# A four-layer graph kernel on one core: rounds per block in the dilation, batch 0's attention beside its preparation, and the order of high and low halves in layer 1

## The chip, the cores and the metric

The kernel runs on one core of a Trainium2 chip. A core has TensorE (PE, matrix products into PSUM), VectorE (DVE), ScalarE (ACT), GpSimd (POOL) and SyncE (SP, which here only issues DMAs). The metric is device time of one execution in microseconds (us); the number that counts is the median of several runs.

## What is computed

Input: features x of 16 batches, 1024 nodes, 128 columns; symmetric 0/1 adjacencies of 16 x 1024 x 1024 with a full diagonal and about 6% ones; a node mask of ones. Each of four layers is a residual and a layer norm, `x = layernorm(x + layer(x, adj))`. The three that matter here:

Layer 0, a gated attention. The score is symmetric, so one product with a fixed matrix gives it.

```python
h = x @ W_w.T + W_b
e = einsum('bjl,bkl->bjk', h @ A, h);  e = e + swapaxes(e, 1, 2)
att = softmax(where(adj > 0, e, -9e15), axis=1) * adj
h_prime = relu(einsum('bij,bjk->bik', att, h))
coeff = sigmoid(concatenate([x, h_prime], -1) @ gate_w.T + gate_b)
return coeff * x + (1 - coeff) * h_prime
```

Layer 1 first thins the adjacency ("dilation"), row after row, each row seeing what earlier rows removed:

```python
def step(carry, n):
    row = carry[n]; num = row.sum()
    sf = where(num > 10, (num + 1) // 2, 1)
    rm = row & (cumsum(row) % sf == 0) & (num > 1)
    carry = carry.at[n].set(row & ~rm)
    carry = carry.at[:, n].set(carry[:, n] & ~rm)
```

and then applies three graph convolutions `out = (adj_d @ x / deg) @ Wr + x @ Wx + b`, each normalized by rows and over the batch. Layers 2 and 3 (a second gated attention and a graph convolution) are not touched by the change.

## The kernel before, in words

**One program, static order.** Everything is unrolled Python that issues instructions to five engines through a tile framework. The framework sets the waits, and it also places the instructions of an engine: the order in the program acts as a priority, and the trace shows instructions of a later stream ahead of those of an earlier one where their inputs are ready. Streams of work are Python generators. `take_turns` (L811) steps several of them alternately; `in_rounds` (L815) steps each one when it is due, and a value that it yields is the number of rounds that it then pauses.

**Layer 0.** `before(s, b)` (L923) prepares a batch: it loads the features xn (L926) and, in eight steps `it`, a block of 128 adjacency rows each (L931), converts it to fp8 on ScalarE (L932, the tile named carry), and checks that the adjacency is symmetric and binary on VectorE (L937, and L945 on PE's transposes, L944). Beside this, at `it == 2` it turns xn into xT (PE L759, ScalarE L951); at `it == 4` it makes G, the scores' right-hand side (PE L766, ScalarE L955, with M0, a product of raw weights made at L894 to L909), and the gate's first half (L775, L777, L780, L958); at `it == 5` it makes hn (PE L963, VectorE L964). `attention(s, b)` (L968) takes eight column blocks: mask (ScalarE L981), score product (PE, called at L982, recorded at L724), masked minimum (VectorE L984), exponential (ScalarE L986), scaling by the sum (L988, L990), and one block later the product with the weights (PE L974). `after(s, b)` (L999) gates and normalizes, and stores. Batch 0's preparation has a call of `in_rounds` of its own (L1024); then batch b's attention runs with batch b+1's preparation and batch b-1's `after` (L1025 to L1032). The raw weights lie in a pool that is opened and closed (L894) on the same side of SBUF on which the work pool is opened next (L910). The PSUM pool ps_h (L892) has two buffers, shared by the weights' products, the transposes and all products of the preparation.

**The dilation.** The 1024 rows are cut into eight blocks k of 128, the 16 batches into two groups g of eight: 16 steps in the order k0g0, k0g1, k1g0 and so on. Within a block the rows depend on each other, so `fixed_point` (L1080) solves for the counts by iteration. One evaluation (L1090) is: thr (L1092), mid = (sk == thr), over 128 x 1024 elements (L1097), eight column sums on PE (pd, L1100), and the new counts ti (L1104); for the last two blocks also even (L1095) and eight more sums (L1102). EVALS, 6 for all blocks, is the number of evaluations. Afterwards VectorE compares the last two iterates (L1107, tile bad) and writes negc, posc and wid, the last at L1130. `removal` (L1133) then applies one batch's block: ranks by products with a step matrix (PE L1144, L1142), two ScalarE passes (L1145), keep (VectorE L1148, L1149), and the mirror of the new rows into the columns (PE L1152 to L1156, ScalarE L1157). `prepare` (L1048) makes sk for the same group's next block. `take_turns` runs the fixed point of step i beside the eight removals of step i-1 and the `prepare` of step i+1 (L1190 to L1193). The first fixed point runs beside the last batch's `after` (L1174).

**The flag.** At the end bad and other conditions are reduced to one number; if it is not zero, a second, general kernel runs (L1842).

**Layer 1.** PE multiplies fp32 features in two passes: `split` (L1268) makes hi, a rounded copy (ScalarE L1272), and lo, the rest (VectorE L1273); lo has a single buffer. `widened` (L1286) makes eight pieces of the adjacency, alternately by ScalarE (L1295) and VectorE (L1293). `adjacency_product` (L1298) has two halves h of 512 columns; for each of a half's four pieces it issues two products with hi, then two with lo (L1306). It is called once in `first` (L1415) for each batch, and once in `keep` (L1482) for each batch in the first two convolutions: 48 times.

Of the kernel before, what the change touches and what calls it, by code (L numbers as in the profile page):

```python
# [17 lines left out]
OP = mybir.AluOpType  # L18
# [6 lines left out]
BIG = 2.0 ** 53  # L25
LN_EPS = 1e-5
BN_EPS = 1e-5
EVALS = 6
GB = 8
QB = 4  # L30

# [608 lines left out]
def fast_kernel(ctx: ExitStack, tc: tile.TileContext, t: dict, out: bass.AP, flag: bass.AP):  # L640

    nc = tc.nc
    B, N, D = t["x"].shape
    NT = N // P
# [42 lines left out]
    def nat(ap):  # L687
        return ap.rearrange("(t p) d -> p t d", p=P)
# [12 lines left out]
    def matrix(pool, src, name, bufs=1):  # L701
        v = pool.tile([P, P], F32, name=name, bufs=bufs)
        nc.sync.dma_start(v, src)
        return v

    def transposed(pool, psum, src, name, tag="tr"):
        v = pool.tile([P, P], F32, name=name)
        p = psum.tile([P, P], F32, name="wtr", tag=tag)
        nc.tensor.transpose(p, src, identf)
        nc.vector.tensor_copy(v, p)  # L710
        return v
# [16 lines left out]
    def tiles3(ap):  # L728
        return ap.rearrange("p (t d) -> p t d", d=P)
# [85 lines left out]
    def in_rounds(streams):  # L815

        due, r = [0] * len(streams), 0
        while any(streams):
            for i, s in enumerate(streams):
                if s is not None and due[i] <= r:  # L820
                    pause = next(s, 0)
                    if pause == 0:
                        streams[i] = None
                    else:
                        due[i] = r + (pause or 1)
            r += 1
# [64 lines left out]
    ps_a = ending.enter_context(tc.tile_pool(name="l0_pa", bufs=1, space=PSUM, reuse_waits="tile"))  # L891
    ps_h = ending.enter_context(tc.tile_pool(name="l0_ph", bufs=2, space=PSUM, reuse_waits="tile"))  # L892

    with tc.tile_pool(name="l0_raw", bufs=1) as raw:  # L894
        W0 = matrix(raw, t["L0_gnn_W_w"], "l0W")
        W0T = transposed(wts, ps_h, W0, "l0WT", "h")
        As0 = symmetric(raw, ps_h, matrix(raw, t["L0_gnn_A"], "l0A"), "l0As", "h")
        AW = raw.tile([P, P], F32, name="l0AW")
        p = ps_h.tile([P, P], F32, name="wtr", tag="h")
        nc.tensor.matmul(p, As0, W0, start=True, stop=True)  # L900
        nc.vector.tensor_copy(AW, p)
        M0 = wts.tile([P, P], F32, name="l0M")
        p = ps_h.tile([P, P], F32, name="wtr", tag="h")
        nc.tensor.matmul(p, W0, AW, start=True, stop=True)
        nc.vector.tensor_copy(M0, p)
        nu = wts.tile([P, 1], F32, name="l0nu")
        p = ps_h.tile([P, 1], F32, name="wtr", tag="h")
        nc.tensor.matmul(p, AW, column(raw, t["L0_gnn_W_b"], "l0b"), start=True, stop=True)
        nc.vector.tensor_scalar(nu, p, -1.0, None, op0=OP.mult)  # L909
# [6 lines left out]
        nc.sync.dma_start(gw[:, :, 0], t["L0_gnn_gate_w"].rearrange("o (h d) -> d (o h)", d=P))  # L916
    gb = row_bcast(wts, t["L0_gnn_gate_b"], 1, "l0gb")
    gbh = wts.tile([P, 1], F32, name="l0gbh")
    nc.vector.tensor_scalar(gbh, gb, 0.5, None, op0=OP.mult)
    nbig = wts.tile([P, 1], F32, name="l0nbig")  # L920
    nc.vector.memset(nbig, BIG)

    def before(s, b):  # L923

        s.xn = work.tile([P, NT, P], F32, name="xn", bufs=3)
        nc.sync.dma_start(s.xn, nat(t["x"][b]))  # L926
        yield 1
        for it in range(NT):
            c = b * NT + it
            an = early.tile([P, N], F32, name="an", bufs=3)  # L930
            nc.sync.dma_start(an, t["adj"][b][it * P:(it + 1) * P, :])  # L931
            nc.scalar.activation(Y[b][:, it, :], an, AF.Copy, accum_out=deg[:, c:c + 1], saturate=False)  # L932

            chk = early.tile([P, N], FP8, name="chk")
            done = (it + 1) * P
            if done < N:
                nc.vector.scalar_tensor_tensor(chk[:, done:], an[:, done:], 0.0, an[:, done:], op0=OP.is_gt,  # L937
                                               op1=OP.not_equal, accum_out=other[:, b, it:it + 1], saturate=False)
            for h in range(it // 4 + 1):
                js = range(4 * h, min(4 * h + 4, it + 1))  # L940
                k = slice(js[0] * P, (js[-1] + 1) * P)
                pt = ps_h.tile([P, 512], F32, name="pt", tag="h")
                for i, jt in enumerate(js):
                    nc.tensor.matmul(pt[:, i * P:(i + 1) * P], Y[b][:, jt, it * P:done], identb, start=True, stop=True)  # L944
                nc.vector.scalar_tensor_tensor(chk[:, k], pt[:, :k.stop - k.start], 0.0, an[:, k], op0=OP.is_gt,  # L945
                                               op1=OP.not_equal, accum_out=other[:, b, 7 + it + 4 * h:8 + it + 4 * h],
                                               saturate=False)
            if it == 2:
                s.xT = work.tile([P, N], F32, name="xT", bufs=2)
                for p, c, _ in turned(ps_h, s.xn):  # L950
                    nc.scalar.copy(s.xT[:, c], p)  # L951
            elif it == 4:
                s.G = work.tile([P, N], F32, name="G", bufs=2)
                for p, c in products(ps_h, (M0, s.xT)):
                    nc.scalar.activation(s.G[:, c], p, AF.Identity, scale=-1.0, bias=nu)  # L955
                pz = gates(ps_h, early.tile([P, N], FP8, name="chk").bitcast(F32), (gw[:, 0, :], s.xT))
                s.gx = small.tile([P, NT], F32, name="gx")
                nc.vector.tensor_copy(s.gx.rearrange("p (q t) -> p q t", t=2), pz[:, :, :, 0])  # L958
            elif it == 5:
                s.hn = work.tile([P, N], F32, name="hn")  # L960
                for p, c, blocks in halves(ps_h):
                    for i, k in enumerate(blocks):
                        nc.tensor.matmul(p[:, i * P:(i + 1) * P], s.xT[:, k * P:(k + 1) * P], W0T, start=True, stop=True)  # L963
                    nc.vector.tensor_add(tiles3(s.hn[:, c]), tiles3(p), b0[:, None, :].to_broadcast([P, 4, P]))  # L964
            yield 2
        nc.gpsimd.dma_start(adj8_d[b], Y[b].bitcast(F32))
# [54 lines left out]
        yield  # L1021

    state = [Batch() for _ in range(B)]
    in_rounds([before(state[0], 0)])  # L1024
    for b in range(B):  # L1025
        streams = []
        if b < B - 1:
            streams.append(before(state[b + 1], b + 1))
        streams.append(attention(state[b], b))
        if b:  # L1030
            streams.append(after(state[b - 1], b - 1))
        in_rounds(streams)  # L1032
    scores.close()

    with ExitStack() as ph:
# [44 lines left out]
        def fixed_point(st, k, g):  # L1080
# [6 lines left out]
            nc.vector.tensor_scalar(v1m, l1, 0.5, -0.5, op0=OP.mult, op1=OP.add)  # L1087
            ti = tiny.tile([P, GB], I32, name="ti")
            nc.vector.tensor_copy(ti, v1m)
            for e in range(EVALS):  # L1090
                thr = tiny.tile([P, GB], I32, name="thr")
                nc.vector.tensor_scalar(thr, ti, 1, None, op0=OP.bitwise_or)  # L1092
                if st.with_last:
                    even = tiny.tile([P, GB], BF16, name="even")
                    nc.vector.tensor_tensor(even, thr, ti, op=OP.is_equal)  # L1095
                mid = sb.tile([P, GB, P], FP8, name="mid")
                nc.vector.tensor_tensor(mid, st.sk, per_member(thr), op=OP.is_equal, saturate=False)  # L1097
                pd = ps_d.tile([P, GB], F32, name="pd")
                for i in range(GB):
                    nc.tensor.matmul(pd[:, i:i + 1], mid[:, i, :], onec, start=True, stop=not st.with_last)  # L1100
                    if st.with_last:
                        nc.tensor.matmul(pd[:, i:i + 1], st.last[:, i, :], even[:, i:i + 1], start=False, stop=True)  # L1102
                tn = tiny.tile([P, GB], I32, name="ti")
                nc.vector.tensor_tensor(tn, pd, v1m, op=OP.add)  # L1104
                prev, ti = ti, tn
                yield
# [151 lines left out]
    with ExitStack() as ph:  # L1258
# [39 lines left out]
        def adjacency_product(pieces, parts):  # L1298

            for h in range(H2):  # L1300
                acc = ps_a.tile([P, 512], F32, name="acc")
                for i in range(NT // 2):
                    for p, part in enumerate(parts):
                        for j in range(2):
                            jt = 2 * i + j
                            nc.tensor.matmul(acc, part[:, jt, :], pieces[h * NT // 2 + i][:, j, :],  # L1306
                                             start=(jt == 0 and p == 0), stop=(jt == NT - 1 and p == 1))
                yield acc, slice(h * 512, (h + 1) * 512)

        def home(b):  # L1310
# [178 lines left out]
        before = None  # L1489
# [5 lines left out]
        for l in range(3):  # L1495
# [42 lines left out]
            before = step  # L1538
# [7 lines left out]
    with ExitStack() as ph:  # L1546
# [7 lines left out]
        W2T, b2, As2, gw, gb, nbig, blcol, Wl = l2.W2T, l2.b2, l2.As2, l2.gw, l2.gb, l2.nbig, l2.blcol, l2.Wl  # L1554
# [247 lines left out]
        state = l2.state  # L1802
# [63 lines left out]
```

## Time and profile before

| | |
|---|---|
| median of 3 runs | 2735.02 us (2731.83 to 2736.03) |
| the profiled execution's own time | 2734.11 us |
| its span, first to last instruction | 2732.4 us |
| mean granted TensorE clock | 0.976 |
| busy: PE, PEld, DVE, ACT, POOL | 93%, 62%, 77%, 72%, 12% |
| layer 0 | 0 to about 649 us |
| dilation (first to last L1097, then the last removals) | 649.9 to about 1022 us |
| layer 1 | to about 1680 us |
| layers 2 and 3 | to the end |

How to read it: the profile shows one execution. "PE" is TensorE's products, "PEld" its loads of weights, which overlap them. A group line names the source line, the engine, the operation, output and inputs; behind the bar stand busy time, mean duration, idle time of that engine just before such instructions, and what ended it. A line of a stretch gives, after its ends and length, the busy us of PE, PEld, DVE, ACT and POOL, the granted clock, the DMA share and GB/s. A line of the timeline gives start, duration, engine, source line, operation, output and inputs, count, and in brackets the idle time before it and who ended it.

### The profile page before, as it was taken

How to read it: one execution, taken by the hardware profiler on the slowest of the kernel's cores; microseconds unless marked ns; L12 is line 12 of the kernel's file. 1: busy time of each engine (PE TensorE's matmuls, PEld its weight loads, DVE VectorE, ACT ScalarE, POOL GpSimd, SP SyncE). 2: the span in 40 equal slices, each digit the busy share in tenths (PEclk: the TensorE clock that was granted, in tenths of full speed). 3: DMA queues.
4: the chain of work that ended last, by engine and by line, in shares of the span. 5: the costliest groups of instructions: out<-in, count | busy, mean ns of one | idle time of the engine just before them, and what ended most of it. 6: DMA issues, size and time to landing. Idle time of an engine off the chain costs nothing.

```text
span 2732.4 us, 41821 instructions
## 1 busy us (share of the span) xinstructions
PE 2552.2 (93%) x15048; PEld 1688.8 (62%) x15048; DVE 2108.6 (77%) x5650; ACT 1977.0 (72%) x3188; POOL 317.1 (12%) x287
## 2 busy tenths in 40 slices
PE   7999999994899888998999998999999999999986
PEld 3444444442666657887778887456666666666655
DVE  5887778875999986776678877577787787787785
ACT  6888889873888786666655543777777777777773
POOL 0000000003000001121112123001010010001001
PEclk9999999996999999999999999999999999999998
DMA  5455445430000042233356655101222211111100
GB/s 189 162 169 171 165 167 177 157 114 23 2 2 2 2 183 96 94 108 124 132 203 224 254 205 211 39 24 62 70 77 73 90 62 62 62 62 62 46 24 25
DMA packets 120810, 285.38 MB, mean 104 GB/s; under 512 B 12305, under 2 KB 65425, under 8 KB 113425
## 3 DMA queue, kind: packets, MB, share of 16 engines
q1 hardware_dynamic: 101280, 203.33, 22.4%
q0 software_dynamic: 19312, 79.28, 7.5%
q8 instruction: 121, 1.98, 0.3%
q14 instruction: 97, 0.79, 0.1%
HBM read 202.72 MB, written 79.82 MB: 103 GB/s over the span
## 4 chain that ended last, share of the span: by engine, by line
PE 62%; DVE 16%; issue 9%; POOL 5%; ACT 4%; DMA 3%; SPq 0%; POOLq 0%; ACTq 0%; DVEq 0%
PE acc L974 8%; PE ph L1618 8%; PE pmm L724 8%; PE acc L1678 7%; PE ph L766 6%; PE acc L1306 5%; PE ph L759 4%; PE pmm L1690 3%; POOL rn L745 2%; PE ph L1605 2%; PE ph L1432 2%; DVE mid L1097 2%; POOL ln_rstd L745 1%; PE s L1144 1%; DVE keep L1148 1%
## 5 line engine op out<-in xcount | busy, mean ns | idle before, releaser
L745 POOL TENSOR_TENSOR ln_rstd<-ln_rstd,mhalf 128x8 f32<-128x8 f32 (+1 forms) x68 | 108.3, 1592 | 1347.6 <-DVE ln_rstd L742 879.7
L974 PE MATMUL acc<-em,hs 128*128 128x512 f32 x512 | 260.1, 607 | 1.9 <-DVE past L1075 1.3
L724 PE MATMUL pmm<-xT,G 128*128 128x512 f32 x512 | 261.8, 604 | 0.0
L1678 PE MATMUL acc<-ex,hs 128*128 128x512 f32 x512 | 248.9, 596 | 7.4 <-DVE hs L1705 4.5
L801 ACT ACTIVATE xn<-xn,ln_nb,ln_rstd 128x128 f32<-128x128 f32 x512 | 204.6, 481 | 70.3 <-DVE ln_nb L799 70.3
L1306 PE MATMUL acc<-a,lo 128*128 128x512 f32 x768 | 240.4, 398 | 15.3 <-DVE lo L1273 15.3
L1306 PE MATMUL acc<-a,hi 128*128 128x512 f32 x768 | 241.4, 399 | 3.8 <-ACT hi L1272 3.6
L986 ACT ACTIVATE em<-em,mx 128x1024 f32<-128x1024 f32 x128 | 146.4, 1144 | 63.5 <-DVE mx L984 63.0
L1698 ACT ACTIVATE ex<-em,mn 128x1024 f32<-128x1024 f32 x128 | 146.8, 1147 | 44.6 <-DVE mn L1695 43.9
L984 DVE CUSTOM_DVE_ANT_0 em<-pmm,msk 128x1024 f32<-128x1024 f32 x128 | 156.0, 1219 | 27.0 <-PE pmm L724 26.4
L1306 PEld LDWEIGHTS acc<-a,lo 128*128 128x128 f32 x768 | 144.3, 190 | 52.2 <-DVE lo L1273 22.6
L1690 PE MATMUL pmm<-G,hT 128*128 128x512 f32 (+3 forms) x416 | 175.3, 523 | 0.1
L1695 DVE CUSTOM_DVE_ANT_0 em<-pmm,msk 128x1024 f32<-128x1024 f32 x128 | 155.3, 1214 | 24.4 <-PE pmm L1692 22.3
L1306 PEld LDWEIGHTS acc<-a,hi 128*128 128x128 f32 x768 | 144.1, 191 | 34.1 <-ACT hi L1272 4.6
L1157 ACT ACTIVATE carry<-pc,negone 128x1024 fp8e4<-128x1024 f32 x128 | 140.8, 1114 | 27.0 <-PE pc L1156 21.7
L932 ACT ACTIVATE carry<-an 128x1024 fp8e4<-128x1024 f32 x128 | 134.4, 1050 | 21.7 <-DMA an<-in_adj 20.7
L981 ACT ACTIVATE msk<-carry,l0nbig 128x1024 bf16<-128x1024 fp8e4 x128 | 145.4, 1137 | 0.0
L1618 PE MATMUL ph<-A,hi 128*128 128x512 f32 x512 | 143.1, 420 | 1.2 <-DVE zn L1607 0.7
L1686 ACT ACTIVATE msk<-A,nbig 128x1024 bf16<-128x1024 fp8e4 x128 | 144.1, 1136 | 0.0
L1678 PEld LDWEIGHTS acc<-ex,hs 128*128 128x128 f32 x512 | 88.7, 190 | 76.8 <-issue 54.6
L1295 ACT CAST a<-A 128x1024 fp32r<-128x1024 fp8e4 x96 | 99.1, 1050 | 50.9 <-PE acc L1306 50.9
L1295 ACT CAST a<-carry 128x1024 fp32r<-128x1024 fp8e4 x96 | 99.3, 1049 | 47.6 <-PE acc L1306 47.4
(319 smaller groups left out, 6237.4 us busy)
## 6 DMA issues: line engine op xcount, KB each, us to landing
an<-in_adj SPq DMA_DIRECT2D x128, 512.0 KB, 3.6
adj_d<-carry POOLq DMA_DIRECT2D x16, 1024.0 KB, 4.2
A<-dil_d SPq DMA_DIRECT2D x16, 1024.0 KB, 5.6
rdeg<-rdeg_d SPq DMA_DIRECT2D x32, 512.0 KB, 3.8
A<-adj_d SPq DMA_DIRECT2D x16, 1024.0 KB, 4.8
ag_d<-ag POOLq DMA_DIRECT2D x24, 512.0 KB, 5.0
ag<-ag_d SPq DMA_DIRECT2D x24, 512.0 KB, 5.0
xn<-in_x SPq DMA_DIRECT2D x16, 512.0 KB, 4.3
```

What stands on the lines that cost most here:

```text
L724: nc.tensor.matmul(p[:, h * 512:(h + 1) * 512], lhsT, rhs[:, h * 512:(h + 1) * 512], start=True, stop=True)
L745: nc.gpsimd.tensor_tensor(r, r, mhalf[:, :n], op=OP.pow)
L766: nc.tensor.matmul(p, W, x[:, c], start=(i == 0), stop=(i == len(pairs) - 1))
L801: nc.scalar.activation(r[:, k.start + i, :], r[:, k.start + i, :], AF.Identity, scale=rstd[:, i:i + 1], bias=nb[:, i:i + 1])
L974: nc.tensor.matmul(s.acc[:, c], hs, em[:, c], start=(jt == 0), stop=(jt == NT - 1))
L984: nc.vector.tensor_tensor_reduce(em, e, msk, 1.0, 3.0e38, op0=OP.add, op1=OP.min, accum_out=mn)
L1295: nc.scalar.copy(a, A[:, 2 * i:2 * i + 2, c])
L1306: nc.tensor.matmul(acc, part[:, jt, :], pieces[h * NT // 2 + i][:, j, :], start=(jt == 0 and p == 0), stop=(jt == NT - 1 and p == 1))
L1618: nc.tensor.matmul(p, part[:, jt, :], A[jt][:, c], start=(jt == 0 and i == 0), stop=(jt == NT - 1 and i == 1))
L1678: nc.tensor.matmul(s.acc[:, c], hs, ex[:, c], start=(jt == 0), stop=(jt == NT - 1))
L1690: nc.tensor.matmul(e[:, c], s.hT[:, js], s.G[:, c], start=True, stop=True)
L1695: nc.vector.tensor_tensor_reduce(row, e, msk, 1.0, 0.0, op0=OP.add, op1=OP.min, accum_out=mn)
```

## The change

There are four edits. EVALS becomes a list with an entry for each block. The pool of raw weights moves to the other side of SBUF, and the scaling of the gate's bias, gbh, moves from before the first batch to after the first call of `in_rounds`. For batch 0 alone, xT, G with the gate's half, and hn are made at `it` 0, 1 and 2 instead of 2, 4 and 5, and the first call of `in_rounds` now takes three streams: batch 0's preparation, its attention from round 8, and batch 1's preparation from round 16; the loop starts at batch 1. In `adjacency_product`, half 0 issues the products with lo one piece later than those with hi: hi 0, hi 1, lo 0, hi 2, lo 1, hi 3, lo 2, lo 3.

```diff
-EVALS = 6
+EVALS = 2, 3, 4, 7, 7, 3, 3, 9
...
-    with tc.tile_pool(name="l0_raw", bufs=1) as raw:
+    with tc.tile_pool(name="l0_raw", bufs=1, side="right") as raw:
...
     gbh = wts.tile([P, 1], F32, name="l0gbh")
-    nc.vector.tensor_scalar(gbh, gb, 0.5, None, op0=OP.mult)
...
-            if it == 2:
+            if it == (2 if b else 0):
                 s.xT = work.tile([P, N], F32, name="xT", bufs=2)
...
-            elif it == 4:
+            if it == (4 if b else 1):
                 s.G = work.tile([P, N], F32, name="G", bufs=2)
...
-            elif it == 5:
+            if it == (5 if b else 2):
                 s.hn = work.tile([P, N], F32, name="hn")
...
-    in_rounds([before(state[0], 0)])
-    for b in range(B):
+    in_rounds([before(state[0], 0), chain([8], attention(state[0], 0)), chain([16], before(state[1], 1))])
+    nc.vector.tensor_scalar(gbh, gb, 0.5, None, op0=OP.mult)
+    for b in range(1, B):
...
-            for e in range(EVALS):
+            for e in range(EVALS[k]):
...
-                for i in range(NT // 2):
-                    for p, part in enumerate(parts):
-                        for j in range(2):
-                            jt = 2 * i + j
-                            nc.tensor.matmul(acc, part[:, jt, :], pieces[h * NT // 2 + i][:, j, :],
-                                             start=(jt == 0 and p == 0), stop=(jt == NT - 1 and p == 1))
+                late = 0 if h else 1
+                for i in range(NT // 2 + late):
+                    for part, k in zip(parts, (i, i - late)):
+                        for jt in range(2 * k, 2 * k + 2) if 0 <= k < NT // 2 else ():
+                            nc.tensor.matmul(acc, part[:, jt, :], pieces[h * NT // 2 + k][:, jt - 2 * k, :],
+                                             start=(part is parts[0] and jt == 0), stop=(part is parts[1] and jt == NT - 1))
```

## The prediction, before the result was known

> **What bounds the kernel now.** I read the page first: the busy tenths in 40 slices of 68 us.
>
> ```profile
> PE   7999999994899888998999998999999999999986
> DVE  5887778875999986776678877577787787787785
> ACT  6888889873888786666655543777777777777773
> PEclk9999999996999999999999999999999999999998
> ```
>
> Slices 1 to 9 (layer 0) have TensorE full, VectorE and ScalarE not; slices 10 to 14 (the dilation) are the only ones with VectorE at 9; from slice 15 (layer 1) TensorE is full again. The change touches the first microseconds of the first stage, all of the second and the products of the third, so I took each alone.
>
> The dilation, by stretches: busy us of PE, PEld, DVE, ACT, POOL.
>
> ```profile
> 753.00:774.00 21.00, 18.91 (x253) 13.49 (x251) 20.14 (x58) 18.24 (x25) 0.00 (x0) 1.00 0.00 1
> 1007.00:1022.00 15.00, 12.49 (x135) 9.02 (x134) 7.93 (x14) 14.73 (x21) 0.06 (x1) 0.96 0.72 285
> ```
>
> With six evaluations beside a set of eight removals VectorE is 96% busy, ScalarE 87%. In the last stretch removals run alone, and ScalarE is the full one, 98%: that shows the next limit. There the ends of carry (L1157) come 2.17 us apart, so eight removals cost 17.4 us at least.
>
> One evaluation in the timeline (start, duration):
>
> ```profile
> 768.15 0.17 DVE L1092 TENSOR_SCALAR thr<-ti 128x8 int32<-128x8 int32 x1
> 768.35 1.23 DVE L1097 TENSOR_TENSOR mid<-sk,thr 128x1024 fp8e4<-128x1024 f16 x1
> 769.63 0.35 PE L1100 MATMUL pd<-onec,mid 128*128 128x1 bf16 x8
> 770.10 0.15 DVE L1104 TENSOR_TENSOR ti<-pd,v1m 128x8 int32<-128x8 f32 x1
> ```
>
> It is serial: 2.13 us from thr to the next thr (770.28). The last instruction of each fixed point is the write of wid, L1130; its spacing is the period of a step:
>
> ```profile
> 671.43 0.16 DVE L1130 TENSOR_SCALAR wid<-hw 128x8 f32<-128x8 f32 x1
> 715.87 0.17 DVE L1130 TENSOR_SCALAR wid<-hw 128x8 f32<-128x8 f32 x1
> 841.58 0.17 DVE L1130 TENSOR_SCALAR wid<-hw 128x8 f32<-128x8 f32 x1
> 862.48 0.17 DVE L1130 TENSOR_SCALAR wid<-hw 128x8 f32<-128x8 f32 x1
> 1004.23 0.17 DVE L1130 TENSOR_SCALAR wid<-hw 128x8 f32<-128x8 f32 x1
> ```
>
> 862.48 - 841.58 = 20.9 us is the steady step; the other ends are at 690.30, 736.85, then every 20.9 to 883.37, then 904.94, 929.52, 957.26, 980.25.
>
> The start of layer 0:
>
> ```profile
> 7.04 0.15 DVE L919 TENSOR_SCALAR l0gbh<-l0gb 128x1 f32<-128x1 f32 x1 [4.13 <-DMA l0gb<-in_L_gnn_gate_b]
> 13.53 0.38 SPq L926 DMA_DIRECT2D xn<-in_x  x1
> 17.88 1.94 PE L759 MATMUL ph<-identf,xn 128*128 128x128 f32 x8 [3.08 <-DMA xn<-in_x]
> 28.57 1.14 PE L724 MATMUL pmm<-xT,G 128*128 128x512 f32 x2
> ```
>
> VectorE stands 4.13 us at a tiny constant; the features xn, first in the program, are fetched only at 13.53, after three adjacency tiles; attention's first product starts at 28.57. PE is busy 1.14, 4.88 and 7.44 us in the first three tens: 16.5 of 30 us idle. From 30 to 50 it idles 1.3, after that almost nothing until 624.
>
> Layer 1: what still stops PE there is the low half.
>
> ```profile
> 1034.17 1.22 PE L1306 MATMUL acc<-a,lo 128*128 128x512 f32 x2 [2.93 <-DVE lo L1273]
> 1094.89 0.73 PE L1306 MATMUL acc<-a,lo 128*128 128x512 f32 x2 [0.20 <-DVE lo L1273]
> 1249.40 0.74 PE L1306 MATMUL acc<-a,lo 128*128 128x512 f32 x2 [1.00 <-DVE lo L1273]
> ```
>
> lo has one buffer, so its 1.22 us subtraction starts only when the last product is done with the old one. All such waits come to 15.3 us (the page, L1306 lo).
>
> **What the Trainium skill says.** "VectorE: DVE Perf Modes", the TRN2 errata section, gives a full-rate fp32 tensor_tensor as (N+151)/0.96 GHz: 1224 ns for N = 1024. mid, of mixed 16 and 32-bit inputs, takes 1219 here: it runs at that rate, and its price is fixed. "PSUM — Partial Sum Buffer", Engine vs sequencer instructions: the ScalarE and VectorE queues are strict FIFO; the trace agrees, since the constant at 7.04 held everything behind it. "Perfetto Trace Analysis", Optimization Strategy: a kernel can have several regimes, each with its own most-contended engine, and interleaving them can pay. The slices show three.
>
> **Part 1, rounds per block (L1090).** For two groups 6 becomes 2, 3, 4, 7, 7, 3, 3, 9: 30 evaluations go, 10 come, 96 to 76. An evaluation occupies VectorE from thr to mid 0.20, mid to the next start 1.14, ti 0.08: 1.42 us; in the last two blocks even adds 0.08, 1.50. Eight pd matmuls go from PE (0.35 us). Where VectorE is the limit that is the worth of one; the floor below is ScalarE's 17.4, which I raise to 18.3 because prepare's 64 small matmuls also run between the removals (bounds 17.4 and 20.9).
> - First fixed point, beside only layer 0's tail on VectorE: 4 x 1.42 = -5.7.
> - Next two ends, 671.43 to 715.87, 44.4 us: then two removal sets of 18.3, and some 4 us to fill the pipe (estimate from ScalarE's 3.19 us of normalizing at 669.31): 40.6, -3.8.
> - Third: 21.0 to 18.3, -2.7. Two steps with 4: 20.9 - 2.84 = 18.1, say 18.5: -4.8.
> - Four steps with 7: +1.42 each, +5.7.
> - Block 5: 20.9 and 21.6 to 18.3: -5.9. Block 6: 24.6 and 27.7, three evaluations of 1.50 each; in the second PE's clock is also down: -4.5 and -6.
> - Block 7: three more each. At best 1.50 (VectorE), at worst 2.9, the spacing of evaluations in the last step now (996.10 to 999.05), when the serial chain is the limit: +4.5 to +8.7 a step. I take 5.5: +11.
> Sum -16.7; with 17.4 as floor and 4.5 in block 7 some -26, with a floor near 20 about -5.
> Will the rounds suffice? Running the recursion in integers on the reference's inputs, the most a block needs, with the round that confirms, is 1, 1, 3, 5, 5, 2, 1, 5, inside the new numbers. If not, the flag (L1842) starts the general kernel.
>
> **Part 2, batch 0.** The raw weights on the right side no longer share the work pool's memory, so xn's load need not wait for them: it can be issued near 4.14, ahead of the adjacency, at the price of 0.4 us of SP's time and its 512 KB before theirs. gbh's 0.15 us passes three streams on VectorE; its first reader is the first after's tanh, tens of us later: nothing. xT (8 transposes, 1.94 us, two ScalarE copies of 0.59), G (4 products, 3.78 us; two 0.69 us copies; gates, 1.08 us) and hn (16 products, 1.97 us; two 0.69 us adds) move ahead of four, three, three adjacency tiles' work on PE, VectorE and ScalarE. They still need M0, at 13.3 now, and ps_h's two buffers. If M0's chain stays where it is, xT is through at 15 or 16 and G at 20, against 28.4. The row of attention is not new: msk of batch 0 already ran at 11.96, so the framework pulls it forward, and the delays of 8 and 16 rounds only set priorities. SP's loads of batch 1 and POOL's store of adj8 keep their order; both are governed by the same buffers. PE work is unchanged, so the gain is idle time: of 17.8 us before 50, the first 11 stay unless M0's chain moves; of the other 7 most goes. I take -6. Ends: -12 (M0's chain too, as nothing holds VectorE at 7.04) and +2 (batch 1's preparation, left alone for its last rounds, leaves PE holes).
>
> **Part 3, the low half.** In half 0 PE does two more high matmuls before the first low ones: 2 x 0.226 us (the spacing in these runs) = 0.45 us of cover. Wait by wait, the smaller of wait and 0.45: seven of 0.2 = 1.4; five of 1.0 and six of 0.53 to 2.37 and the first 2.93 = 12 x 0.45 = 5.4. Sum -6.8; I take -6.5. Nothing is added. Best -12, if the filler it displaces also fits; worst +3. After this the next late thing is the product's own buffer (ag, 1.4 to 1.8 us, five times), untouched.
>
> **Sum.** -16.7 - 6 - 6.5 = -29.2. The profiled execution took 2734.11 (span 2732.4 and 1.7 around it), 0.9 under the median of 2735.02: 2734.1 - 29.2 = 2704.9, so 2705.
>
> **Rivals.**
> - **All works better**: floor 17.4 (-24), M0's chain early (-12), low half -7: 2691. For: ScalarE at 98% alone. Against: PE at 18.9 of 21 in the steady step.
> - **Layer 0 gives nothing**, because attention was already pulled forward and adjacency, not features, sets the pace: 2711. For: msk at 11.96. Against: PE's 3.08 us wait for xn.
> - **Removals set the pace (slower)**: in the dilation, the 20.9 us come from the loop through ScalarE, PE and keep, and VectorE only looks full. Then of 30 removed evaluations only the first four pay (-5.7), while 10 added ones take a slot of 2.9: +29. With parts 2 and 3 that is +10.8: 2745. It decides from where the other 26 return under 10.8/26 = 0.42 us each. Against: ScalarE's 17.4 alone.
> - **The low half backfires**: the second high piece is made by VectorE, and if it queues behind lo, 48 products lose up to 0.45 us: 2705 + 6.5 + 21.6 = 2733, no change. Against: pieces are cast a product ahead.
>
> **Chances.** Forecast 0.52, better 0.18, layer 0 nothing 0.17, removals 0.05, low half 0.05, a mix of weak gains 0.02, rounds too few 0.01. About 0.2% (5.5 us) is what a measurement here can tell from no change. Faster 0.89, same 0.05 (the low half), slower 0.06. The range 2684 to 2726 takes in the first three cases with the bounds of the floor and of block 7.
>
> **What would show it.** Right: L1097 x76; wid 18 to 18.6 us apart in blocks 1, 2 and 5 with ScalarE above 95%, 22.3 in blocks 3 and 4; xn issued before 5 us, the first pmm near 20; waits of L1306 on lo near 8 us. Wrong: periods near 20.9 with fewer rounds; block 7 steps above 32 us; PE idle between 30 and 70 us.

## The result, and the profile after

The changed kernel takes 2712.37 us (median of 6 runs, 2710.31 to 2713.94) against 2733.25 of the kernel before in the same comparison (2730.95 to 2736.03): ratio 0.9925, 95% interval 0.9914 to 0.9936, so 17.5 to 23.5 us less. The forecast was 2705, some 29 us less, with a range of 2684 to 2726. The profiled execution took 2712.03, span 2710.2.

The busy tenths of the page, 40 slices of 68 us, as before:

```profile
PE   8999999996889879999999998999999999999986
DVE  6887778875799876776688876577877878787785
```

PE begins a tenth higher (the first 68 us). In the dilation the four 9s of VectorE (slices 11 to 14) became 7 9 9 8: it is no longer full throughout. Evaluations are 76, as counted on:

```profile
L1097 DVE TENSOR_TENSOR mid<-sk,thr 128x1024 fp8e4<-128x1024 f16 x76 | 92.8, 1220 | 0.7
```

The ends of fixed points, in the same form as before:

```profile
657.46 0.15 DVE L1130 TENSOR_SCALAR wid<-hw 128x8 f32<-128x8 f32 x1
929.33 0.17 DVE L1130 TENSOR_SCALAR wid<-hw 128x8 f32<-128x8 f32 x1
970.44 0.16 DVE L1130 TENSOR_SCALAR wid<-hw 128x8 f32<-128x8 f32 x1
998.17 0.17 DVE L1130 TENSOR_SCALAR wid<-hw 128x8 f32<-128x8 f32 x1
```

The first comes 14 us earlier (671.43), and the last only 6 us (1004.23): most of the early lead is given back, above all between 929.33 and 970.44, the first step of block 7. A step's length is better read where the removals stand, from the start of the first keep (L1148) of each set of eight to the next set's. That table, beside the prediction's terms (layer 0's lead is taken at the start of the power of deg, L1183, 627.96 before and 624.35 after):

| stretch of the dilation | before, us | after, us | change | predicted |
|---|---|---|---|---|
| layer 0's end to the first keep, 4 evaluations fewer | 47.0 | 34.9 | -12.1 | -5.7 |
| next two steps, 6 to 2 and to 3 | 44.2 | 45.2 | +1.0 | -3.8 |
| third, 6 to 3 | 21.0 | 20.0 | -1.0 | -2.7 |
| two with 4 | 41.9 | 41.1 | -0.8 | -4.8 |
| blocks 3 and 4, four with 7 | 83.6 | 90.6 | +6.9 | +5.7 |
| block 5, two with 3 | 41.8 | 39.0 | -2.9 | -5.9 |
| block 6, two with 3 | 50.3 | 42.8 | -7.5 | -10.5 |
| block 7, two with 9 | 47.4 | 61.5 | +14.0 | +11 |
| the last removals | 15.8 | 17.1 | +1.3 | 0 |
| sum | | | -1.1 | -16.7 |

So in its own stage part 1 brought one microsecond. A second profile of each kernel (below) has every step of the dilation before within 0.3 us of the first, and the end of the dilation after within 0.3 us too, so this table is no chance.

Part of the first row only moved into the second. The 3.19 us in which ScalarE normalizes layer 0's last batch stood before the first keep (669.31); now they stand behind it (662.28), in a step of 25.2 us where before it was 20.9.

Layer 0, in the timeline of after:

```profile
4.14 0.43 SPq L925 DMA_DIRECT2D xn<-in_x  x1
6.89 0.15 DVE L1024 TENSOR_SCALAR l0gbh<-l0gb 128x1 f32<-128x1 f32 x1 [3.94 <-DMA l0gb<-in_L_gnn_gate_b]
12.39 1.96 PE L759 MATMUL ph<-identf,xn 128*128 128x128 f32 x8
19.26 1.13 PE L724 MATMUL pmm<-xT,G 128*128 128x512 f32 x2
```

The features are issued at 4.14, attention's first product starts at 19.26 instead of 28.57. The constant gbh still stands at the front of VectorE, waiting 3.94 us, though the program now writes it after the first call of in_rounds: the framework placed it early. PE idles 9.8 us in the first 30 (before 16.5), but 3.2 between 30 and 70 (before 1.3) and 1.9 between 70 and 620 (before 0.02).

Layer 1, the groups of the page (busy, mean ns, idle before and its releaser). Before, the second line stood at 240.4 and 15.3, and the first at 241.4 and 3.8:

```profile
L1306 PE MATMUL acc<-a,hi 128*128 128x512 f32 x768 | 233.7, 398 | 12.0 <-DVE a L1293 9.0
L1306 PE MATMUL acc<-a,lo 128*128 128x512 f32 x768 | 230.1, 394 | 5.8 <-DVE lo L1273 5.8
```

The waits on lo fell by 9.5. The idle time before the high half rose by 8.2, and 9.0 of it now ends with a piece cast by VectorE. So the two together fell only by 1.3, while the busy time of both fell by 18.

### The profile page after: what moved, and what is told of

Read it like the earlier page. It is cut to its first block, busy times and chain, and to the rows that moved or that the text cites. A ratio compares the mean times of both kernels' runs of the same rounds, so it can differ in the third digit from the quotient of the medians.

```text
span 2710.2 us, 41446 instructions
## 1 busy us (share of the span) xinstructions
PE 2540.1 (94%) x14888; PEld 1677.4 (62%) x14888; DVE 2085.2 (77%) x5590; ACT 1977.6 (73%) x3188; POOL 317.9 (12%) x287
## 4 chain that ended last, share of the span: by engine, by line
PE 56%; DVE 16%; issue 7%; POOL 5%; ACT 4%; DMA 3%; POOLq 0%; ACTq 0%; DVEq 0%
PE ph L1618 8%; PE acc L1678 7%; PE acc L1306 6%; PE ph L766 5%; PE acc L973 5%; PE pmm L724 5%; PE ph L759 4%; PE ph L1432 3%; PE pmm L1690 3%; PE ph L1605 2%; DVE mid L1097 2%; DVE keep L1148 2%; POOL rn L745 2%; POOL ln_rstd L745 1%; ACT q L1145 1%
## 5 line engine op out<-in xcount | busy, mean ns | idle before, releaser
L1306 PE MATMUL acc<-a,hi 128*128 128x512 f32 x768 | 233.7, 398 | 12.0 <-DVE a L1293 9.0
L1306 PE MATMUL acc<-a,lo 128*128 128x512 f32 x768 | 230.1, 394 | 5.8 <-DVE lo L1273 5.8
L1306 PEld LDWEIGHTS acc<-a,hi 128*128 128x128 f32 x768 | 142.2, 189 | 43.5 <-DVE a L1293 11.5
L1306 PEld LDWEIGHTS acc<-a,lo 128*128 128x128 f32 x768 | 143.3, 189 | 41.1 <-DVE lo L1273 11.5
```

The costliest lines, as they stand in the source:

```text
L1306: nc.tensor.matmul(acc, part[:, jt, :], pieces[h * NT // 2 + k][:, jt - 2 * k, :], start=(part is parts[0] and jt == 0), stop=(part is par ...
```

## The experiments

All in the order in which they ran. A version's time, and its ratio, stand beside runs of the kernel before on the same chip; versions from e5 on ran on other chips than e4, so their distance from e4 is good to about two us.

**One part at a time.** Each of the three parts put alone into the kernel before; the edits are those of the change.

e1_rounds, the list of rounds:
```diff
-EVALS = 6
+EVALS = 2, 3, 4, 7, 7, 3, 3, 9
```


> The kernel before with the list of rounds alone (2, 3, 4, 7, 7, 3, 3, 9). The prediction's sum: -16.7, about 2716.5. The reading by stages of the two traces (what the dilation gained in its first fixed point, some 10 us, it lost again by its end): -1, so 2732, with the last keep (L1148) at about 1020 instead of 1021.0, the steps of block 7 near 33 and 29 us, and the steps of few evaluations near 20.0.

Measured: 2725.99 against 2732.09, ratio 0.9976 (0.9967 to 0.9985), so -6.6 with -9.0 to -4.1. The prediction's -16.7 is outside the interval. Its dilation is nearly that of after: last keep at 1019.58, -1.4, steps of block 7 32.8 and 28.7; two steps are 1.1 shorter than in after (24.1 and 21.8 in place of 25.2 and 22.9). Most of the gain lies at the start of layer 1, which the edit does not touch. From the last keep to the 65th product of L1306, the kernel before and then e1 (length, busy us of PE, PEld, DVE, ACT, POOL, granted clock):

```profile
1021.03:1063.34 42.31, 33.84 (x265) 27.62 (x265) 23.25 (x40) 26.81 (x40) 4.72 (x6) 0.84 0.35 108
```

```profile
1019.58:1057.57 37.99, 32.95 (x266) 26.90 (x265) 23.28 (x40) 25.86 (x39) 4.25 (x6) 0.91 0.15 46
```

That is 4.3 us less: PE idles 5.0 in place of 8.5, and the clock stays low half as long. VectorE's wait of 6.9 us for the degrees (L1400, at 1031.7 before) is gone. The other profiles with six evaluations everywhere (e2, e3, e6 and the second of before) take 42.1 to 43.2, those with the new list (after and its second) 37.5 and 37.0. So this gain belongs to part 1, though no term of the prediction has it; why the new list brings it is not shown.

e2_layer0, batch 0's part alone.

> The kernel before with batch 0's part alone. The prediction's sum: -6, about 2727. The reading by stages: -3.7, about 2729.5, with the power of deg (L1183) starting 3 to 4 us earlier and nothing else moved.

Measured: 2726.99, ratio 0.9982 (0.9973 to 0.999), so -4.9 (-7.4 to -2.7); the power of deg starts 3.8 us earlier than in the profile of before. Between executions that start varies: 627.96 to 629.65 in four profiles with the old layer 0, 623.9 to 625.2 in nine with the new one. The predicted -6 is within.

e3_low, the late low half alone.

> The kernel before with the late low half alone. The prediction's sum: -6.5, about 2727. The reading by stages: -13 to -14, about 2719.5, of which only some 6 us are waits taken away and the rest is TensorE's clock, which fell to 0.5 after stalls near 1034, 1298, 1398 and 1592 us of the profile before. If the clock has nothing to do with the order of the products, the dips stay in this kernel and the gain is 6 to 7 us.

Measured: 2724.58, ratio 0.9972 (0.996 to 0.9983), so -7.7 (-10.9 to -4.6). The prediction's -6.5 holds, not the reading by stages. Its profile has no drop of the clock between 1040 and 1600; what that means is taken up with the second profiles.

The three sum to -19.2, the whole change gave -20.5 by its ratio: the parts add.

**The added evaluations taken back.** e4_no_more, on the changed kernel:
```diff
-EVALS = 2, 3, 4, 7, 7, 3, 3, 9
+EVALS = 2, 3, 4, 6, 6, 3, 3, 6
```


> The changed kernel with the 10 added evaluations taken back: EVALS 2, 3, 4, 6, 6, 3, 3, 6. By the prediction's prices of added evaluations (5.7 for blocks 3 and 4, 11 for block 7): 2712.4 - 16.7 = 2695.7. By the trace, in which block 7's two steps grew by 14 us and those of blocks 3 and 4 by some 8: about 2690. If the time of these steps is set by the loop of removals or by something else than the number of evaluations: 2712 to 2706.

Measured: 2693.27, ratio to before 0.9856 (0.9841 to 0.987): 19 us faster than the changed kernel. Block 7's steps went from 32.8 and 28.6 to 25.4 and 22.9 (-13.1), blocks 3 and 4 from 90.6 to 85.8 (-4.8), the last removals from 17.1 to 15.6. So the ten added evaluations cost 19; the thirty removed ones bring about 25, where the prediction's terms have 33.4.

**As few as the inputs need.** e5_few:
```diff
-EVALS = 2, 3, 4, 7, 7, 3, 3, 9
+EVALS = 1, 1, 3, 5, 5, 2, 1, 5
```


> The changed kernel with as few evaluations as these inputs need: EVALS 1, 1, 3, 5, 5, 2, 1, 5; 20 fewer than the list 2, 3, 4, 6, 6, 3, 3, 6, which gave 2693.3. If an evaluation is worth 1.42 us of VectorE wherever it stands, as the prediction priced it: -28, 2665, with steps of blocks 1, 2, 5 near 18. If the steps with few evaluations are bound by the loop of removals (ScalarE, TensorE, keep): blocks 1, 2, 5 and 6 stay where they are (20.0 to 20.9), and only the first fixed point (-2.8), the four steps of blocks 3 and 4 (20.9 to 20.2, -2.8) and the two of block 7 (-2.5 each) gain: -11, 2682.

Measured: 2685.77, ratio 0.9837 (0.9824 to 0.985), -7.5 against e4 for 20 evaluations (by the two ratios -5). Block 7's steps fell to 21.6 and 21.0 (-5.7 together), the first keep by 2.0. The steps of block 2, with one evaluation fewer than in e4, take 21.3 in place of 20.2 and 20.9, and the four of blocks 3 and 4, with one fewer each, 84.5 in place of 85.8. The two of block 1, with one evaluation each, still take 19.5 and 20.4. The price of 1.42 wherever an evaluation stands has fallen.

**What of layer 0's part carries its gain.** e6_side, one line of the kernel before:
```diff
-    with tc.tile_pool(name="l0_raw", bufs=1) as raw:
+    with tc.tile_pool(name="l0_raw", bufs=1, side="right") as raw:
```


> The kernel before with the pool of raw weights on the right side alone, nothing else of batch 0's part. If the early load of the features carries that part's gain, most of the 5 us comes with this line: 2727. If the reordering (xT, G and hn at it 0, 1, 2, and the three streams) carries it: -1 or nothing, 2731 to 2733, with xn issued near 4.1 us and the first pmm still past 25.

Measured: 2728.65, ratio 0.9991 (0.9983 to 1.0). The time alone tells little; in the trace the power of deg starts 2.3 us earlier, and the first pmm at 26.04. So, as far as single profiles tell, the early load carries some 2.3 of the 3.8 us and the order of the preparation the rest; neither case as written.

**Which piece VectorE casts.** e7_cast_order, on e4:
```diff
-                    if i % 2:
+                    if i // 2 if h == 0 else i % 2:
```


> The changed kernel with EVALS 2, 3, 4, 6, 6, 3, 3, 6 (2693.3), and in half 0 pieces 0 and 1 cast by ScalarE and 2 and 3 by VectorE, in place of alternately; the same work. If the new waits of hi on VectorE's piece (9.9 us in that kernel's profile) come from the second piece standing behind lo on VectorE, they go, and the time falls by 4 to 9: 2684 to 2689. If VectorE or a DMA is late there in any case, the wait turns up at another tile and the time stays at 2693.

Measured: 2700.5, ratio 0.9884 (0.9869 to 0.9899): 7 us slower than e4. The groups of its page:

```profile
L1306 PE MATMUL acc<-a,lo 128*128 128x512 f32 x768 | 233.1, 398 | 13.0 <-DVE lo L1273 12.9
L1306 PE MATMUL acc<-a,hi 128*128 128x512 f32 x768 | 234.0, 399 | 3.2 <-ACT hi L1272 3.2
```

The wait on the piece is gone and stands at lo again. So which engine casts the piece is not the cause, and the second case of the expectation is what happened, only that the exchange is a loss. The cause is one step back on VectorE, which a period of the changed kernel shows:

```profile
1276.95 0.27 DVE L1400 TENSOR_REDUCE nodeg<-d 8x1 f32<-8x128 f16 x1 [2.76 <-DMA d<-row]
1280.07 0.69 DVE L1293 CAST a<-A 128x1024 fp32r<-128x1024 fp8e4 x1
1280.81 1.19 PE L1306 MATMUL acc<-a,hi 128*128 128x512 f32 x4 [1.64 <-DVE a L1293]
1286.80 0.73 PE L1306 MATMUL acc<-a,lo 128*128 128x512 f32 x2 [0.49 <-DVE lo L1273]
```

VectorE stands 2.76 us for the degrees' way through memory (d), and seven operations that are queued behind it, the cast of the piece last, come late. All six waits on a piece in the changed kernel follow such a wait of VectorE (2.4 to 2.8 us) by some 4 us. In the kernel before the same delay (2.37 us at 1287.63) ended elsewhere, in two waits of PE:

```profile
1295.84 0.73 PE L1281 MATMUL acc<-A,step 128*32 128x256 fp8e4 x20 [1.51 <-DVE ag L1483]
1297.58 0.73 PE L1306 MATMUL acc<-a,lo 128*128 128x512 f32 x2 [1.01 <-DVE lo L1273]
```

1.51 + 1.01 = 2.52 before, 1.64 + 0.49 = 2.13 after: the late low half saves 0.4 of it, what the prediction gave it, and the rest changed its name. Over the six such periods the waits come to 15.2 us before and 11.8 after.

**gbh off VectorE.** e8_gbh_pool, on e4:
```diff
-    nc.vector.tensor_scalar(gbh, gb, 0.5, None, op0=OP.mult)
+    nc.gpsimd.tensor_scalar(gbh, gb, 0.5, None, op0=OP.mult)
```


> The changed kernel with EVALS 2, 3, 4, 6, 6, 3, 3, 6 (2693.3), and gbh scaled by GpSimd in place of VectorE, so that nothing on VectorE stands behind the load of the gate's bias. If M0's chain on VectorE waits for that constant, the first pmm comes 2 to 4 us earlier (16 to 17) and the time falls by 1 to 4: 2689 to 2692. If the weights' own loads set M0: no change, 2693.

Measured: 2696.13, ratio 0.9868 (0.9853 to 0.9883): no gain over e4. Its timeline:

```profile
4.45 0.28 DVE L832 TENSOR_TENSOR l0As<-l0A,wtr 128x128 f32<-128x128 f32 x1
9.80 1.09 DVE L936 SCALAR_TENSOR_TENSOR chk<-an 128x896 fp8e4<-128x896 f32 x1 [5.07 <-DMA an<-in_adj]
10.82 0.29 DVE L901 COPY l0AW<-wtr 128x128 f32<-128x128 f32 x1
12.21 0.16 DVE L909 TENSOR_SCALAR l0nu<-wtr 128x1 f32<-128x1 f32 x1
12.44 1.96 PE L759 MATMUL ph<-identf,xn 128*128 128x128 f32 x8
```

The start of M0's chain, l0As, moved from 8.46 (in after) to 4.45, but its next step (L901) is queued behind the check of an adjacency tile, which waits for its load until 9.80: a wait took the place of the wait. So M0's chain ends hardly earlier than without the edit, and the run doesn't tell what an earlier M0 would bring. That it would bring something is likely, because the features are not late. Their load (issued at 4.12, the view of tile xn from 4 to 5 us):

```profile
DMA to landing us min/median/max: 4.4/4.4/4.4
```

They are there near 8.5. The transposes stand at 12.4 in both kernels, in PE's queue behind M0's products and released by l0nu, with which VectorE ends M0's chain. Some 3.9 us (12.44 less 8.5, an estimate) are open there.

**What lifts the floor of a step.** e9_prep_pe, on e4, with the flag set to zero:
```diff
-                    for kb in range(NT):
-                        m = step0 if kb == k else twos[:, :P if kb < k else 1]
-                        nc.tensor.matmul(s0[:, i, :m.shape[1]], Y[b0 + i][:, kb, ks], m, start=(kb == 0), stop=(kb == NT - 1))
+                    nc.tensor.matmul(s0[:, i, :], Y[b0 + i][:, k, ks], step0, start=True, stop=True)
```


> The changed kernel with EVALS 2, 3, 4, 6, 6, 3, 3, 6 (2693.3), leaving out seven of the eight products of each member in prepare (8 of 64 matmuls a step stay) and the flag's value (it is set to zero), so its counts are not the reference's. If TensorE's share of prepare is what lifts the loop of removals from 17.4 to 20.0 a step: the steps of blocks 1, 2 and 5 fall to 18 to 18.5, and the whole by 10 to 15, to about 2680. If it hides behind other waits: those steps stay at 20, 2690 to 2693.

Measured: 2672.26, ratio 0.9782 (0.9765 to 0.9798), 21 us faster than e4. From the first keep to the last the dilation takes 312.7 in place of 336.6 us. A stretch of e4 (two steps, of blocks 1 and 2: length, busy us of PE, PEld, DVE, ACT, POOL):

```profile
723.60:763.60 40.00, 34.53 (x454) 25.48 (x453) 34.14 (x101) 34.92 (x48) 0.00 (x0) 1.00 0.01 2
```

In e4 no engine is full: PE 86%, VectorE 85%, ScalarE 87%. In e9, between 704.4 and 742, VectorE is busy 36.9 of 37.6 us: it does more evaluations in the shorter time.

But the edit takes away more than PE's work. Among the seven products are those that read the row blocks which earlier removals changed; the one that stays reads only block k's own. So in e9 a fixed point no longer waits for the removals before it, and it runs up to two steps ahead. Here the last one ends 33 us before its removals begin; in e4 these two lie 1.0 us apart (979.47 and 980.50):

```profile
923.67 0.17 DVE L1128 TENSOR_SCALAR wid<-hw 128x8 f32<-128x8 f32 x1
956.92 0.75 DVE L1146 TENSOR_SCALAR keep<-q,wid 128x1024 fp8e4<-128x1024 f16 x1 [0.88 <-ACT q L1143]
```

Block 7's steps fall most, from 25.4 and 22.9 to 17.8 and 17.4, and they show that the gain is not that of the products: in e9 no evaluation is left in them (six each in e4), and the second of them has no product of prepare in e4 either. Those of blocks 1 and 2 come to 18.4 to 21.0, not to the 18 to 18.5 expected, with VectorE full. So the run doesn't price prepare's products.

e10_prep_none, on e4: prepare's tiles are filled by GpSimd (`nc.gpsimd.memset(st.sk[:, qs, :], 3.0)` and the like).

> The same kernel (2693.3), leaving out prepare on TensorE and VectorE altogether (its tiles are filled with constants by GpSimd; the flag's value is set to zero), so that only removals and evaluations are left beside each other. If prepare as a whole is the excess over 17.4: steps with 2 to 4 evaluations 17.4 to 18.3, steps with 6 some 18.5 to 19 (20.9 less about 2 of VectorE), the whole about 2655 to 2665. If removals beside evaluations lose time in the loop of queues without it: still 19 to 20 with few evaluations, the whole 2680 or more.

Measured: 2666.39, ratio 0.9761 (0.9745 to 0.9777). The sets of removals up to block 4 take 19.2 to 20.7 with few and many evaluations alike, since here too fixed points no longer wait for removals and run ahead; VectorE is busy 38.7 of 39.4 us there (698.7 to 738.1). From block 5 on no evaluation is left beside the removals, and a step takes 17.4 to 17.8:

```profile
895.00:930.00 35.00, 28.16 (x275) 19.90 (x273) 19.59 (x38) 34.98 (x50) 0.00 (x0) 1.00 0.00 1
```

ScalarE is full (34.98 of 35): 17.4 is the floor of eight removals alone, as predicted. Step for step the run doesn't compare with e4, as its fixed points have moved. Beside e5, whose steps of block 1 with one evaluation take 19.5 and 20.4, it says that prepare and one evaluation together lift a step by some 2 to 3 us.

**Second profiles.** e11_before_again and e12_after_again, both kernels unchanged.

> The kernel before, unchanged, for a second profile. If the drops of the granted clock in layer 1 (near 1298, 1398 and 1592 us) belong to the order of the products, they come back at the same places. If they depend on how a stall falls against the clock's own window, they lie elsewhere or are missing, and layer 1 differs by 2 to 6 us between two executions of the same kernel.

> The changed kernel, unchanged, for a second profile: the same two cases as for the second profile of the kernel before. From the first case layer 1 is 557 us from its first to its last product of L1306, as in the first profile; from the second, 557 to 562.

Measured: 2728.89 and 2713.7. From the last keep to the start of the last product of L1306 the kernel before took 578.5 and then 576.0 us, the changed one 564.4 and 566.2. The drops of 1298, 1397 and 1592 are missing in the second profile of before; two others have come, at 1274.7 and 1373.7: the second case. The drop at 1298.39, the stretch ahead of it and itself (the third number from the right is the granted clock), and the stretch ahead of the one at 1274.72 in the second profile:

```profile
1294.98:1298.39 3.41, 1.54 (x24) 1.12 (x24) 3.41 (x6) 1.05 (x1) 0.00 (x0) 1.00 0.00 0
1298.39:1301.80 3.41, 3.41 (x10) 2.67 (x9) 1.03 (x2) 1.21 (x2) 0.59 (x1) 0.50 0.86 276
```

```profile
1271.31:1274.72 3.41, 1.44 (x23) 1.07 (x23) 3.41 (x6) 1.05 (x1) 0.00 (x0) 1.00 0.00 0
```

A pair of waits of PE, on ag and on lo, stands in both stretches ahead. Each of the two profiles has five such pairs, near 1248, 1272, 1297, 1322 and 1347 us, and only one of the five was followed by a drop: the third in the first profile, the second in the other.

## Why the prediction was right, and where its steps were wrong

The time came into the range because two parts were priced about rightly, and because the wide range took in a third part, the largest, of which only two fifths came (-6.6 of -16.7). Even of that, most (4.3 us) came at the start of layer 1, where the prediction had nothing for this part: that is luck. Of its signs of being wrong all three showed: periods of 20 to 21 us with fewer rounds, a step of 32.8 us in block 7, and PE idle between 30 and 70 us.

**Part 2 (-6), right in size.** Measured alone -4.9. The idle time of PE fell in the first 30 us by 6.7, as worked out. Of this 1.9 came back between 30 and 70, which the prediction had named as a sign against it, and another 1.9 between 70 and 620. The end of -12, with M0's chain early too, stays open: e8 freed the head of VectorE's queue, but the chain then met the next wait in it.

**Part 3 (-6.5), right in size, not wait by wait.** Measured alone -7.7 (-10.9 to -4.6). From the 65th product of L1306 to the last, PE idles 24.5 to 25.9 us in five profiles with the old order (before, its second, e1, e2, e6) and 19.3 to 21.5 in six with the new one (after, its second, e3, e4, e5, e8): some 4 to 5 us, at the near end of what was timed. The seven waits of 0.2 us, counted at 1.4, did not go. After has eight of them, and the batches of `first` take the same time: 86.8 us from the 257th product to the 513th in before and after. The wait of 2.93 at 1034 went with part 1's list; in e3, which has the new order alone, 2.23 of it is left. What the order did shorten is the periods of VectorE's delay. The rival that it backfires at VectorE's piece named a wait that did come (9.0 us), but that wait is the old delay under another name. Adding up waits of the two halves, before 19.1 and after 17.8, would show a gain of 1 and miss the rest.

**The clock.** Between the first profiles layer 1 gained 14.1 us, twice what part 3 gives. 4.8 of it is the start, up to the 65th product, which belongs to part 1. Another part is the clock: in the rest, PE's busy time at half clock costs 6.5 us before and nothing after; in the second profiles 3.4 and 1.7. With this taken off, the old order takes 529.7 to 531.5 us in its five profiles, the new one 526.2 to 528.4 in its six, so 3 us are the order's own and the rest of the 14.1 is the start and chance.

The Trainium skill, "TensorE: Matmul & The Clock Gate", section "What's actually happening", says that the array falls to half its clock after an idle window of about 3.4 us, and that this window runs freely, so that the same kernel can meet it differently. The trace agrees with the half, with the length and with the chance. Two products with lo take 0.85 us from start to start in the drop, where they take 0.46 at full clock; the drop lasts 3.41 us, and the others in layer 1 last as long or two to four times that; and the same waits led to one at another place in the second profile. It doesn't agree that the window must be idle: PE was busy 1.54 of the 3.41 us ahead of the drop, and its longest wait was 1.51. Whether the late low half also makes drops rarer is open: from 1040 to 1600 the old order's profiles (before, its second, e1, e2, e6) have 3, 2, 3, 1 and 1 of them, the new order's (after, its second, e3, e4, e5, e8) 0, 1, 0, 2, 2 and 2, too few to tell.

**Part 1 (-16.7), wrong: -1.1 in the dilation, -6.6 timed.** Term by term:
- *The first fixed point, 4 x 1.42 = -5.7.* It gave -12.1 at the first keep. The step that failed is to price an evaluation by the time it occupies VectorE. There it is on the path with its whole round, from mid over PE to the next mid: before, the starts of mid from the second evaluation to the sixth lie at 655.48 to 665.92, 2.6 us apart, and 4 x 2.6 is 10.4. VectorE was not idle meanwhile; layer 0's tail filled it, but the first keep didn't have to wait for that tail, and 3.2 us of it only moved into the next step. The stretch in the kernel before:

```profile
655.00:666.00 11.00, 1.78 (x34) 1.17 (x32) 10.74 (x37) 0.00 (x0) 0.00 (x0) 0.50 0.00 1
```

- *The floor of 18.3 a step.* This is the term that made the forecast too large: the removals of evaluations after the first fixed point were to give -27.7 and gave -11.2. Most steps with few evaluations take 19.9 to 21.1 (one of block 5 17.9, one of block 6 22.9, and the one with layer 0's tail 25.2), near the upper bound of 20.9 that stood beside it. The prediction gave what stands beside the removals 0.9 us; by e5 and e10 prepare and one evaluation together take 2 to 3. In after's steps from 684.5 to 724.5 PE, VectorE and ScalarE are busy at most 88%, 81% and 90%, so no engine's full load sets them. In the same steps of e4 (683.65 to 723.58), along the chain of work followed back from the last instruction, ScalarE's passes, keep, the removals' products and carry follow one another; prepare's products have 4% of that chain, its sk on VectorE 5%, mid and pd 13%. Which of these would have to go for 18.3 is not shown: e9 and e10 change what waits for what as well, and the number of buffers between PE and ScalarE was not varied.
- *Blocks 3 and 4, +5.7.* Measured +6.9, right: with seven evaluations VectorE is the limit again (93 to 98% busy in these steps).
- *Block 7, +11.* Measured +14.0, and +1.3 in the last removals: 7.6 a step, inside the bounds of 4.5 and 8.7 but near the upper one. It is the serial chain: in the first step ScalarE waits 8.7 us for negc, the removals being long done. The clock fell there as well, to 0.66 between 955 and 975, but the evaluations that run alone in that stretch are no slower (mid starts at 959.2, 962.1 and 964.5, so 2.9 and 2.4 us apart, against 2.95 in the last step before), so it is hardly the cause.

**The rivals.** "Removals set the pace" had much of the mechanism of the floor: the 26 later evaluations gave 11.2 us, 0.43 each, at its very point of 0.42. Its time of 2745 did not come, because the first four gave 12.1 and not 5.7, and the ten added ones cost 22 by the table and 19 by e4, not 29. "All works better" fell with the floor, M0's part of it untested. "Layer 0 gives nothing" fell with e2.

**Better than both.** The changed kernel with EVALS 2, 3, 4, 6, 6, 3, 3, 6 (e4) takes 2693.27, 1.4% under the kernel before. It has one evaluation more than these inputs need in blocks 3, 4 and 7, where the change has two, two and four.

## What to carry to other kernels

Price an operation by where it stands. In a serial chain that others wait for it costs its whole round (2.6 us here), even where its engine is busy with other work in between. On a full engine it costs about its own busy time (1.2 to 1.7 in blocks 3 and 4). In a step that a round through several queues sets it costs next to nothing (0.43). One number for all three was the error here. When an engine at 96% is relieved, don't take the busiest remaining engine's load as the next floor: add up what stands in every queue that the loop passes, helpers included. When a product is left out to find its price, ask first which waits go with it. And compare two profiles stage by stage only after a second profile of the same kernel has shown how much that stage varies.

## What was not expected of the hardware

- Two profiles of one kernel agree within 0.3 us over the whole dilation, yet differ by 2.5 us in the next stage, through drops of TensorE's clock at other places.
- Two waits of PE of 1.5 and 1.0 us within 3.3 us were enough to lose the full clock once, and four other such pairs in the same profile were not; the products then ran at about half rate for 3.4 us.
- Cut into stretches of 3.41 us that end where the clock falls, the 14 profiles show this between 20 and 2600 us: every stretch at full clock in which PE was busy less than 44% was followed by one at half clock, and none in which it was busy more than 63%. Between these both occur.
- One evaluation fewer can lengthen a step: block 2 takes 21.3 us with 3 evaluations (e5) and 20.2 and 20.9 with 4 (e4). Why is open.
